# Mamba layer of a four-layer hybrid: a buffer for the logarithm, merged silus, other slots for the turning of states, another order for the first chunk

## The chip, the core and the metric

One core of one Trainium2 chip, float32 throughout. The time is device microseconds of one execution of the whole program. The core has five engines, each with its own in-order queue: TensorE (PE; its weight loads are the row PEld), VectorE (DVE), ScalarE (ACT), GpSimd (POOL) and SyncE (SP), whose queue issues most transfers.

## The reference, cut to what matters

The program computes four layers on an image tensor of 2 x 256 x 32 x 32: layer 0 is a pair of Mamba blocks, layer 1 a large-kernel convolution attention, layers 2 and 3 attention with mixtures of experts. Only layer 0 is touched by the change. It starts with a group norm, and then each Mamba block (512 inner channels, 16 states) does this on the 1024 tokens of each of two images:

```python
xs, res = split(u @ in_w + in_b)
xs = silu(conv4(xs) + conv_b)                   # depthwise, four taps, causal
dt, B, C = split(xs @ xproj_w)                  # 16 + 16 + 16
delta = softplus(dt @ dt_w + dt_b)
for t: h = exp(delta_t * A) * h + delta_t * B_t * xs_t ;  y_t = sum over states of h * C_t
y = (y + xs * D) * silu(res);  out = y @ out_w + out_b;  x = x + layernorm(out)
```

## The kernel before

Layer 0 is cut in chunks of 512 tokens: two blocks of four chunks, eight in a row, numbered 0 to 7 here. Chunks 0, 2, 4 and 6 begin an image (no state is read). Channels lie on partitions, as four groups of 128 (`dc` 0 to 3). Each chunk has three parts, written as Python generators that give up control at each `yield`:

- `front(j)`: input product (four groups, `m_in`), convolution as four matmuls by diagonal matrices (`taps`) for each group (`m_conv`), silu (L280), the product with `xproj_w` (`m_xd`), `m_ct` (the C columns), then softplus: |v| into `e` (L316) and relu into `delta` (L317) from PSUM, `e = exp(-e)` (L319, one instruction for all groups), a correction `du` for the rounding of 1 + e (L322, L323), the logarithm in place on `e` (L325), and three additions and products (L328 to L330) that leave delta and `du` = delta * xs. The elementwise steps of L322 to L330 go to POOL, those of chunk 0 to VectorE.
- `scan(j)`: for each state n of 16, `m_b` (one row of B on all partitions, fetched by SP), two halves h(n, 0) and h(n, 1) on POOL (L377, 128 x 1024), and for each group ACT's `m_da` = exp(delta * A) into PSUM (L384, three buffers) and VectorE's scan along time (L388), written scan (n, dc) here. Then each of four pieces of 128 tokens is turned by four PE transposes into PSUM (`m_ht`, L350, written ht(n, i), three buffers), and VectorE adds it, times C, to `m_ya` (L358; L356 for n = 0), written y(n, i). There are five buffers for the halves h, used in turn, and a half is free once all pieces of its n are turned.
- `back(j)`: gate product and silu (L408, L412), sum with the skip path (`m_y`), product with the gate (L427), output product (`m_out`), layer norm (L142 to L147), turning back (L153) and the addition to x (L454, L459).

`scan` weaves the others in. After each scan (n, dc) it takes one step of `between` (for n > 0 and dc < 3: three slots of four, none in n = 0) and then one step of `before`, which turns and adds one piece of the state before:

```python
if n and dc < 3:
    next(between, None)
next(before, None)
```

`between` is a chain: `back` of the last chunk, `front` of the next one, then seven steps of `aside` (small products for layer 1's taps: `w1t`, `taps_ps`). The framework's scheduler then settles each engine's final order when the program is built: it follows the order of writing, but puts an instruction that it holds ready ahead of one that it holds waiting. What stands where on each engine is read from the built program.

Pools that matter: `m_one` has one buffer a tag (`pre`, which is also `e`; `gate`; `o`), `m_mm` has two PSUM buffers for all small products, `m_da` three, `m_ht` three. An activation function from another table set than the last one needs a table load on ACT (`ACT_TABLE_LOAD`).

Before chunk 0, SP issues the loads in the order columns, rows, four tiles of x, weights; the group norm of both images runs, and then the front of chunk 0, alone.

Of the kernel before, what the change touches and what calls it, by code (L numbers as in the profile page):

```python
# [9 lines left out]
F32 = mybir.dt.float32  # L10
# [52 lines left out]
class Net:  # L63


    def __init__(self, ctx, tc, cols, rows):
        self.tc, self.nc = tc, tc.nc
        nc = self.nc
        const = ctx.enter_context(tc.tile_pool(name="const", bufs=1))
        self.small = ctx.enter_context(tc.tile_pool(name="small", bufs=4))  # L70
        self.cols = const.tile([P, NCOLS], F32, name="cols_sb")
        nc.sync.dma_start(self.cols, cols)
        self.rows = const.tile([P, NROWS], F32, name="rows_sb")
        nc.sync.dma_start(self.rows, rows.partition_broadcast(P))
        self.ident = const.tile([P, P], F32, name="ident")
        make_identity(nc, self.ident)
        self.eps5 = const.tile([P, 1], F32, name="eps5")
        nc.vector.memset(self.eps5, 1e-5)
        self.eps6 = const.tile([P, 1], F32, name="eps6")
        nc.vector.memset(self.eps6, 1e-6)  # L80
        self.one = const.tile([P, 1], F32, name="one")
        nc.vector.memset(self.one, 1.0)
        self.ones_row = const.tile([1, P], F32, name="ones_row")
        nc.vector.memset(self.ones_row, 1.0)

# [73 lines left out]
def group_norm(net, pool, psum, u, x):  # L159

    nc = net.nc
    grp = pool.tile([P, P], F32, name="gn_grp")
    nc.vector.memset(grp, 0.125)
    g3 = grp.rearrange("p (g j) -> p g j", j=8)
    nc.gpsimd.affine_select(
        out=g3, in_=g3, compare_op=ALU.is_ge, fill=0.0, base=0,
        pattern=[[-8, 16], [0, 8]], channel_multiplier=1,
    )
    nc.gpsimd.affine_select(
        out=g3, in_=g3, compare_op=ALU.is_ge, fill=0.0, base=7,  # L170
        pattern=[[8, 16], [0, 8]], channel_multiplier=-1,
    )
    n = NCC * NB
    mv = pool.tile([P, n, 2], F32, name="gn_mv")
    for cc in range(NCC):
        for b in range(NB):
            st = net.small.tile([P, 2, 6], F32, name="gn_st")
            for h in range(2):
                nc.vector.bn_stats(out=st[:, h, :], in_=x[:, cc, b, h * 512 : (h + 1) * 512])
            nc.vector.bn_aggr(out=mv[:, cc * NB + b, :], in_=st.rearrange("p h s -> p (h s)"))  # L180
    means = pool.tile([P, n], F32, name="gn_means")
    nc.vector.tensor_copy(means, mv[:, :, 0])
    ps = psum.tile([P, TC], F32, tag="mm", name="gn_ps")
    nc.tensor.matmul(ps[:, :n], lhsT=grp, rhs=means, start=True, stop=True)
    gm = pool.tile([P, n], F32, name="gn_gm")
    nc.vector.tensor_copy(gm, ps[:, :n])

    d = pool.tile([P, n], F32, name="gn_d")
    nc.vector.tensor_sub(d, means, gm)
    nc.vector.tensor_mul(d, d, d)  # L190
    nc.vector.tensor_add(d, d, mv[:, :, 1])
    ps = psum.tile([P, TC], F32, tag="mm", name="gn_ps2")
    nc.tensor.matmul(ps[:, :n], lhsT=grp, rhs=d, start=True, stop=True)
    rs = pool.tile([P, n], F32, name="gn_rs")
    net.rstd(rs, ps[:, :n])
    for b in range(NB):
        for cc in range(NCC):
            i = cc * NB + b
            nc.vector.tensor_scalar(
                u[:, cc, b, :], x[:, cc, b, :], gm[:, i : i + 1], rs[:, i : i + 1],  # L200
                ALU.subtract, ALU.mult,
            )


class Mamba:
# [10 lines left out]
    def load(self):  # L216
        net, nc, m, wpool = self.net, self.net.nc, self.m, self.wpool
        in_w, out_w, xproj_w, dt_w = self.weights
        self.in_sb = wpool.tile([P, NCC, DI], F32, tag="in_w", name=f"{m}_in_sb")
        nc.sync.dma_start(self.in_sb, in_w[:, :, :DI])  # L220
        self.xp_sb = wpool.tile([P, NDC, XD], F32, tag="xproj_w", name=f"{m}_xp_sb")
        nc.sync.dma_start(self.xp_sb, xproj_w)
        self.dt_sb = wpool.tile([RANK, DI], F32, tag="dt_w", name=f"{m}_dt_sb")
        nc.sync.dma_start(self.dt_sb, dt_w)
        self.gate_sb = wpool.tile([P, NCC, DI], F32, tag="gate_w", name=f"{m}_gate_sb", bufs=2)
        nc.sync.dma_start(self.gate_sb, in_w[:, :, DI:])
        self.out_sb = wpool.tile([P, NDC, C], F32, tag="out_w", name=f"{m}_out_sb", bufs=2)
        nc.sync.dma_start(self.out_sb, out_w)

        self.taps = wpool.tile([P, NDC * 4, P], F32, tag="taps", name=f"{m}_taps")  # L230
        self.skip = wpool.tile([P, NDC, P], F32, tag="skip", name=f"{m}_skip", bufs=2)
        for i in range(NDC * 4):
            nc.vector.tensor_scalar_mul(
                self.taps[:, i, :], net.ident, net.col(f"{m}_conv_w", i)
            )
        for dc in range(NDC):
            nc.vector.tensor_scalar_mul(self.skip[:, dc, :], net.ident, net.col(f"{m}_D", dc))
        self.aneg = wpool.tile([P, NDC * NS], F32, tag="aneg", name=f"{m}_aneg", bufs=2)
        nc.scalar.activation(self.aneg, net.col(f"{m}_A_log", 0, NDC * NS), AF.Exp)
        nc.vector.tensor_scalar_mul(self.aneg, self.aneg, -1.0)  # L240
        self.state = wpool.tile([P, NS, NDC], F32, tag="state", name=f"{m}_state", bufs=2)
# [5 lines left out]
    def front(self, j, eng=None):  # L247

        net, nc, m, one, two = self.net, self.net.nc, self.m, self.one, self.two
        eng = eng or nc.gpsimd  # L250
# [22 lines left out]
        for dc in range(NDC):  # L273
            ps = self.ps_mm.tile([P, TC], F32, tag="mm", name=f"{m}_conv_{j}_{dc}")
# [5 lines left out]
            nc.scalar.activation(xs[:, dc, :], ps, AF.Silu, bias=net.col(f"{m}_conv_b", dc))  # L280
# [4 lines left out]
        for dc in range(NDC):  # L285
            nc.tensor.matmul(
                ps[:XD, :], lhsT=self.xp_sb[:, dc, :], rhs=xs[:, dc, :],
                start=(dc == 0), stop=(dc == NDC - 1),
            )
        nc.scalar.copy(xd, ps[:XD, :])  # L290
# [16 lines left out]
        e = one.tile([P, NDC, 3 + TC], F32, tag="pre", name=f"{m}_e_{j}")[:, :, :TC]  # L307
        du = two.tile([P, NDC, TC], F32, tag="du", name=f"{m}_du_{j}")
        for dc in range(NDC):
# [7 lines left out]
            nc.scalar.activation(delta[:, dc, :], ps, AF.Relu, bias=b)  # L317
            yield
        nc.scalar.activation(e, e, AF.Exp, scale=-1.0)  # L319
# [5 lines left out]
        nc.scalar.activation(e, e, AF.Ln, bias=net.one)  # L325
        yield
        for dc in range(NDC):
            eng.tensor_add(e[:, dc, :], e[:, dc, :], du[:, dc, :])  # L328
            eng.tensor_add(delta[:, dc, :], delta[:, dc, :], e[:, dc, :])
# [4 lines left out]
    def scan(self, j, before, between):  # L334
# [11 lines left out]
        def add(n, hs, i):  # L346

            ps = self.ps_ht.tile([P, DI], F32, tag="ht", name=f"{m}_ht_{j}_{n}_{i}")
            for dc in range(NDC):
                nc.tensor.transpose(  # L350
                    ps[:, dc * P : (dc + 1) * P], hs[dc // G][:, dc % G, i * P : (i + 1) * P],
                    net.ident,
                )
            c = ct[:, i, n : n + 1]
            if n == 0:
                nc.vector.tensor_scalar_mul(ya[:, i, :], ps, c)  # L356
            else:
                nc.vector.scalar_tensor_tensor(ya[:, i, :], ps, c, ya[:, i, :], ALU.mult, ALU.add)  # L358

# [4 lines left out]
        def rest(n, hs):  # L364
            for i in range(TPC):
                if i == 1 and first:
                    keep(n, hs)
                add(n, hs, i)
                yield

        for n in range(NS):
# [9 lines left out]
            for dc in range(NDC):  # L381
# [9 lines left out]
                if n and dc < 3:  # L391
                    next(between, None)
                next(before, None)
            before = rest(n, hs)
# [4 lines left out]
    def back(self, j):  # L399
# [5 lines left out]
        for dc in range(NDC):  # L405
            ps = self.ps_mm.tile([P, TC], F32, tag="mm", name=f"{m}_g_{j}_{dc}")
            for kc in range(NCC):
# [5 lines left out]
                gate[:, dc, :], ps, AF.Silu, bias=net.col(f"{m}_in_b", NDC + dc)  # L413
            )
            yield

# [46 lines left out]
def layer0(net, x, x_dram, m1, m2, aside):  # L463
# [4 lines left out]
    with (  # L468
# [13 lines left out]
        ]  # L482
        blocks[0].load()
        group_norm(net, wpool, ps_mm, x, x)
        units = [(m, j) for m in blocks for j in range(NCH)]
        for _ in units[0][0].front(0, nc.vector):
            pass
        before, done = iter(()), []
        aside = aside(ps_mm)
        for u, (m, j) in enumerate(units):  # L490
            ahead = units[u + 1 : u + 2]
            if ahead and ahead[0][1] == 0:
                ahead[0][0].load()
            before = m.scan(j, before, chain(*done, *(a.front(k) for a, k in ahead), islice(aside, 7)))
# [5 lines left out]
class Taps:  # L500
# [3 lines left out]
    def __init__(self, net, pool, w1, w2):  # L504
# [3 lines left out]
        nc.sync.dma_start(self.w2_sb, w2)  # L508
# [743 lines left out]
def conv_attn_hybrid(ctx: ExitStack, tc: tile.TileContext, a: dict, out: bass.AP):  # L1252
# [7 lines left out]
    with (  # L1260
# [3 lines left out]
        for cc in range(NCC):  # L1264
            for b in range(NB):
                nc.sync.dma_start(x[:, cc, b, :], a["x"][b, cc])

# [5 lines left out]
            lambda psum: taps.make(psum, conv_dram),  # L1273
# [98 lines left out]
```

## Time and profile before

| | us |
|---|---|
| median of 9 runs | 2614.33 (2604.52 to 2619.06) |
| profiled execution | 2617.87 |
| its span | 2614.3 |
| first scan / first scan of state 1, group 1 | 75.18 / 81.69 |
| end of the last scan and accumulation of layer 0 | some 1204 |
| engines busy in the span: PE, DVE, ACT, POOL | 2140.6, 1479.9, 1033.7, 1068.7 |

The first accumulations of state 0 stand at 81.05, 217.14, 364.32, 507.73, 652.01, 794.22, 938.88 and 1080.60 us: a chunk takes 136 to 147 us. The profile is one execution. A wait is put down to what ended it; a line such as `DVE a L1 <- ACT b L2: 10.0, 4, 3.0` says that VectorE's instruction of line 1 waited 10.0 us for ACT's line 2, in four places, the longest 3.0. In a timeline the first two columns are start and duration in us, `x2` counts instructions put together, and brackets give the idle time before.

### The profile page before, as it was taken

To read this page: it belongs to the slowest core of one execution; us is meant where nothing else is said; L and a number is where in the kernel's file an instruction comes from. 1 tells how busy PE (TensorE), PEld (TensorE's weight loads), DVE (VectorE), ACT (ScalarE), POOL (GpSimd) and SP (SyncE) were. 2 spreads that over 40 slices of the span, in tenths; PEclk is the share of its full clock that TensorE was granted. 3 is DMA by queue.
4 is the path that set the end of the run, shared out by engine and by line. 5 is a ranking of instruction groups with operands and counts; after the bars stand their busy time and mean duration, and the time that the engine had idled before them with its cause. 6 is when DMAs were issued, how large, how long until landed. Compare 5 with 4: busy or idle time off the path is not lost. (4 is left out here: it accounts for less than half of the span.)

```text
span 2614.3 us, 24599 instructions
## 1 busy us (share of the span) xinstructions
PE 2140.6 (82%) x8178; PEld 1309.0 (50%) x8178; DVE 1479.9 (57%) x2232; ACT 1033.7 (40%) x1664; POOL 1068.7 (41%) x708
## 2 busy tenths in 40 slices
PE   5767778696868778777999789949999499689995
PEld 2445445454545454544555556526555267456653
DVE  2879789787979797995002865542222333522222
ACT  3764656666565757561001243312111423211113
POOL 0786766859595867662000620013232000023331
PEclk9767888797878878876998899969999799789997
DMA  3011101101111111110000010038888200178885
GB/s 140 29 47 33 31 33 53 38 27 50 29 49 40 45 37 34 48 53 1 11 6 1 1 41 8 17 141 304 286 291 279 77 1 17 73 250 311 312 283 177
DMA packets 74909, 241.87 MB, mean 93 GB/s; under 512 B 21944, under 2 KB 34621, under 8 KB 62624
## 3 DMA queue, kind: packets, MB, share of 16 engines
q1 hardware_dynamic: 65504, 219.32, 24.6%
q0 software_dynamic: 9024, 20.74, 2.6%
q8 instruction: 65, 1.06, 0.2%
q14 instruction: 60, 0.49, 0.1%
q10 hardware_dynamic: 256, 0.26, 0.0%
HBM read 222.87 MB, written 21.33 MB: 93 GB/s over the span
## 5 line engine op out<-in xcount | busy, mean ns | idle before, releaser
L377 POOL TENSOR_TENSOR m_h<-m_du,m_b 128x1024 f32<-128x1024 f32 x256 | 600.2, 2369 | 341.3 <-PE m_ht L350 157.0
L350 PE MATMUL m_ht<-ident,m_h 128*128 128x128 f32 x2048 | 417.5, 331 | 173.5 <-DVE m_ya L358 95.5
L350 PEld LDWEIGHTS m_ht<-ident,m_h 128*128 128x128 f32 x2048 | 282.2, 167 | 377.5 <-issue 116.9
L384 ACT ACTIVATE m_da<-m_delta,m_aneg 128x512 f32<-128x512 f32 x512 | 349.6, 690 | 265.0 <-DVE m_h L388 260.0
L358 DVE SCALAR_TENSOR_TENSOR m_ya<-m_ht,m_ct,m_ya 128x512 f32<-128x512 f32 x480 | 344.0, 729 | 60.6 <-PE m_ht L350 60.2
L1183 PE MATMUL h<-we,xts 128*128 128x512 f32 x752 | 343.8, 600 | 1.0 <-DVE xts L1173 1.0
L388 DVE TENSOR_TENSOR_SCAN m_h<-m_da,m_state,m_h 128x512 f32<-128x512 f32 x256 | 320.2, 1268 | 38.2 <-ACT m_da L384 26.6
L388 DVE TENSOR_TENSOR_SCAN m_h<-m_da,m_h 128x512 f32<-128x512 f32 x256 | 304.8, 1206 | 56.8 <-ACT m_da L384 37.7
L1155 POOL DMA_INDIRECT x<-l_zd,source x94 | 95.8, 1019 | 510.3 <-DVE source L1119 449.3
L1214 POOL DMA_INDIRECT yd<-y,target x94 | 95.6, 1017 | 347.3 <-DMA yd<-y,target 177.3
L1190 DVE TENSOR_TENSOR hid<-hid,h 128x512 f32<-128x512 f32 x94 | 64.6, 688 | 282.1 <-PE h L1183 282.1
L1183 PEld LDWEIGHTS h<-we,xts 128*128 128x128 f32 x752 | 137.5, 193 | 139.7 <-issue 137.9
L1201 ACT COPY hts<-ht 128x512 f32<-128x512 f32 x94 | 55.1, 586 | 351.0 <-PE ht L1197 351.0
L1208 PE MATMUL o<-we,hts 128*128 128x256 f32 x752 | 184.5, 390 | 1.5 <-ACT hts L1201 1.5
L604 PE MATMUL acc<-act,pair 128*98 128x448 f32 (+14 forms) x448 | 165.3, 517 | 0.0
L1208 PEld LDWEIGHTS o<-we,hts 128*128 128x128 f32 x752 | 139.7, 196 | 19.5 <-ACT hts L1201 1.9
L1213 DVE COPY y<-o 128x256 f32<-128x256 f32 x94 | 39.9, 424 | 149.6 <-DMA yd<-y,target 79.6
L276 PE MATMUL m_conv<-m_pre,m_taps 128*128 128x512 f32 x256 | 115.5, 594 | 3.3 <-ACT m_xs L280 3.2
L604 PEld LDWEIGHTS acc<-act,pair 128*98 128x98 f32 x448 | 73.8, 167 | 70.3 <-issue 54.2
L528 PE MATMUL taps_ps<-w_sb,w1ts 128*128 128x49 f32 x196 | 44.1, 385 | 69.5 <-ACT w1ts L524 69.3
L1189 ACT ACTIVATE hid<-h 128x512 f32<-128x512 f32 x94 | 56.1, 597 | 99.1 <-PE h L1183 98.0
L384 ACT ACT_TABLE_LOAD x69 | 88.5, 1283 | 1.2
(289 smaller groups left out, 3079.6 us busy)
## 6 DMA issues: line engine op xcount, KB each, us to landing
we<-in_l_experts_dram SPq DMA_DIRECT2D x94, 1536.0 KB, 8.4
m_b<-m_bd SPq DMA_DIRECT2D x128, 256.0 KB, 3.2
yl<-yd SPq DMA_DIRECT2D x16, 512.0 KB, 5.0
w<-in_l_w_dram SPq DMA_DIRECT2D x7, 896.0 KB, 6.2
l_zd<-l_z SPq DMA_DIRECT2D x8, 512.0 KB, 2.9
taps<-taps_sb SPq DMA_DIRECT2D x7, 343.0 KB, 3.5
pair<-taps SPq DMA_DIRECT2D x7, 343.0 KB, 3.9
act<-in_x_dram SPq DMA_DIRECT2D x4, 512.0 KB, 7.0
```

Source lines behind the costliest of these rows:

```text
L276: nc.tensor.matmul(ps, lhsT=self.taps[:, dc * 4 + k, :], rhs=pre[:, dc, k : k + TC], start=(k == 0), stop=(k == 3),)
L350: nc.tensor.transpose(ps[:, dc * P : (dc + 1) * P], hs[dc // G][:, dc % G, i * P : (i + 1) * P], net.ident,)
L358: nc.vector.scalar_tensor_tensor(ya[:, i, :], ps, c, ya[:, i, :], ALU.mult, ALU.add)
L377: nc.gpsimd.tensor_mul(h, du[:, g * G : (g + 1) * G, :], b.unsqueeze(1).to_broadcast(half))
L384: nc.scalar.activation(da, delta[:, dc, :], AF.Exp, scale=self.aneg[:, i : i + 1])
L388: nc.vector.tensor_tensor_scan(h, da, h, 0.0 if first else state[:, n, dc : dc + 1], ALU.mult, ALU.add)
L604: nc.tensor.matmul(acc[b, k][:, lo - 16 * k : hi - 16 * k, co : co + n], lhsT=lhsT, rhs=x4[:, kc, b, lo - r0 : hi - r0, ci : ci + n], star ...
L1155: nc.gpsimd.indirect_dma_start(out=x, out_offset=None, in_=zd[:, :], in_offset=bass.IndirectOffsetOnAxis(ap=source[:, g : g + 1], axis=0), ...
L1183: nc.tensor.matmul(ps, lhsT=xt[:, kc * P : (kc + 1) * P], rhs=w12[:, s, kc, :], start=(kc == 0), stop=(kc == NCC - 1),)
L1190: nc.vector.tensor_mul(hid, hid, h[1])
L1208: nc.tensor.matmul(ps[:, :C], lhsT=ht[:, mc * P : (mc + 1) * P], rhs=w[:, 8 + mc, :], start=(mc == 0), stop=(mc == NHC - 1),)
L1214: nc.gpsimd.indirect_dma_start(out=yd[:, :], out_offset=bass.IndirectOffsetOnAxis(ap=target[:, g : g + 1], axis=0), in_=y, in_offset=None, ...
```

## The change

Five edits, all in layer 0. Line numbers of the changed file are some 30 to 50 higher.

1. `ln = Ln(1 + e)` goes to a tile of its own, with the tag of `gate`, right behind the exponential; the correction steps read `e` and come behind it, with the two additions and the product.
2. The four evictions of the convolution and of the gate add their bias with `Identity`, and one `Silu` in place follows over all four groups. Chunk 0 keeps its silus apart.
3. `front` yields in the middle of each convolution group and of the xproj product, and twice for each group of the softplus steps; `scan` gives `between` a step after every scan but the very first.
4. `rest` makes the four transposes of a piece, yields, and adds the piece only when it is called again, after the next scan. `before` is called ahead of `between`, and what is left of the state before is chained.
5. Start: columns and `w2` are issued from ACT's queue, x of image 0 ahead of the weights, x of image 1 and the rows behind; the group norm works by image, that of image 1 behind chunk 0's front; the front of chunk 0 (`alone`) makes groups 1 and 3 of the convolution on VectorE, the relu on VectorE, and Exp and Ln by group.

```diff
 # scan
-                if n and dc < 3:
+                next(before, None)
+                if n or dc:
                     next(between, None)
-                next(before, None)
-            before = rest(n, hs)
+            before = chain(before, rest(n, hs))
 # rest
             for i in range(TPC):
-                if i == 1 and first:
+                ps = self.ps_ht.tile([P, DI], F32, tag="ht", name=f"{m}_ht_{j}_{n}_{i}")
+                for dc in range(NDC):
+                    nc.tensor.transpose(
...
+                yield
+                c = ct[:, i, n : n + 1]
...
+                    nc.vector.scalar_tensor_tensor(
+                        ya[:, i, :], ps, c, ya[:, i, :], ALU.mult, ALU.add
+                    )
+                if i == 0 and first:
                     keep(n, hs)
-                add(n, hs, i)
-                yield
 # front: convolution
+            if alone and dc % 2:
+                nc.vector.tensor_scalar(
...
+                for k in range(1, 4):
+                    nc.vector.scalar_tensor_tensor(
...
+                nc.scalar.activation(xs[:, dc, :], xs[:, dc, :], AF.Silu)
+                continue
...
+                if k == 1:
+                    yield
-            nc.scalar.activation(xs[:, dc, :], ps, AF.Silu, bias=net.col(f"{m}_conv_b", dc))
+            nc.scalar.activation(xs[:, dc, :], ps, AF.Silu if alone else AF.Identity, bias=b)
+            yield
+        if not alone:
+            nc.scalar.activation(xs, xs, AF.Silu)
             yield
 # front: softplus
+        ln = one.tile([P, NDC, TC], F32, tag="gate", name=f"{m}_ln_{j}")
...
-            nc.scalar.activation(delta[:, dc, :], ps, AF.Relu, bias=b)
+            if alone:
+                nc.vector.tensor_scalar(delta[:, dc, :], ps, b, 0.0, ALU.add, ALU.max)
+            else:
+                nc.scalar.activation(delta[:, dc, :], ps, AF.Relu, bias=b)
             yield
-        nc.scalar.activation(e, e, AF.Exp, scale=-1.0)
+        parts = [slice(dc, dc + 1) for dc in range(NDC)] if alone else [slice(0, NDC)]
+        for a in parts:
+            nc.scalar.activation(e[:, a, :], e[:, a, :], AF.Exp, scale=-1.0)
+        for a in parts:
+            nc.scalar.activation(ln[:, a, :], e[:, a, :], AF.Ln, bias=net.one)
         yield
         for dc in range(NDC):
             eng.tensor_scalar(du[:, dc, :], e[:, dc, :], 1.0, -1.0, ALU.add, ALU.add)
             eng.tensor_sub(du[:, dc, :], e[:, dc, :], du[:, dc, :])
             yield
-        nc.scalar.activation(e, e, AF.Ln, bias=net.one)
-        yield
-        for dc in range(NDC):
-            eng.tensor_add(e[:, dc, :], e[:, dc, :], du[:, dc, :])
-            eng.tensor_add(delta[:, dc, :], delta[:, dc, :], e[:, dc, :])
+            eng.tensor_add(ln[:, dc, :], ln[:, dc, :], du[:, dc, :])
+            eng.tensor_add(delta[:, dc, :], delta[:, dc, :], ln[:, dc, :])
             eng.tensor_mul(du[:, dc, :], delta[:, dc, :], xs[:, dc, :])
             yield
 # layer0
+        norm = GroupNorm(net, wpool, ps_mm, x)
         blocks[0].load()
-        group_norm(net, wpool, ps_mm, x, x)
+        load_image()
+        blocks[0].load_rest()
+        net.load_rows()
+        norm.image(0)
         units = [(m, j) for m in blocks for j in range(NCH)]
-        for _ in units[0][0].front(0, nc.vector):
+        for _ in units[0][0].front(0, alone=True):
             pass
+        norm.image(1)
```

## The prediction

> **What bounds the kernel now.** The change touches layer 0 alone, so I read that stretch, 0 to 1204 us of the span. First the table of windows: from 750 to 890 us, one chunk, VectorE is busy 121.32 of 140 us, PE 112.71, POOL 101.86, ACT 86.49. VectorE sets the pace there: a scan and an accumulation follow each other every 1.78 us (1.83 where a state is read), 64 times a chunk. Only what VectorE waits for can be won or lost. The list of waits of layer 0 (waiter, what ended the wait: total us, times, longest) says for whom it waits:
>
> ```profile
> POOL m_h L377 <- PE m_ht L350: 157.0, 43, 8.8
> ...
> DVE m_h L388 <- ACT m_da L384: 64.3, 11, 9.1
> ...
> DVE m_ya L358 <- PE m_ht L350: 60.2, 34, 5.5
> ACT m_e L325 <- POOL m_du L323: 57.5, 7, 9.0
> ...
> DVE m_du L322 <- ACT m_e L319: 35.5, 1, 35.5
> ...
> DVE m_h L388 <- POOL m_h L377: 24.2, 21, 2.9
> ```
>
> ACT's logarithm (L325, in place on e) waits 57.5 us for POOL to have read e, and the exponentials behind it in ACT's queue starve the scans. Then POOL's own timeline over one such place (start, us, line, count):
>
> ```profile
> 446.14 4.67 POOL L377 TENSOR_TENSOR m_h<-m_du,m_b 128x1024 f32<-128x1024 f32 x2 [1.89 <-PE m_ht L350]
> 450.79 3.81 POOL L322 TENSOR_SCALAR m_du<-m_e 128x512 f32<-128x512 f32 x2
> 454.56 2.32 POOL L323 TENSOR_TENSOR m_du<-m_e,m_du 128x512 f32<-128x512 f32 x2
> 456.85 3.81 POOL L322 TENSOR_SCALAR m_du<-m_e 128x512 f32<-128x512 f32 x2
> 460.62 2.31 POOL L323 TENSOR_TENSOR m_du<-m_e,m_du 128x512 f32<-128x512 f32 x2
> 462.88 4.66 POOL L377 TENSOR_TENSOR m_h<-m_du,m_b 128x1024 f32<-128x1024 f32 x2
> 467.50 2.31 POOL L328 TENSOR_TENSOR m_e<-m_e,m_du 128x512 f32<-128x512 f32 x2
> ```
>
> POOL is never idle from 450.79 to 495: while ACT waits for it, POOL is late with the halves h itself. VectorE in the same place:
>
> ```profile
> 457.20 0.72 DVE L358 SCALAR_TENSOR_TENSOR m_ya<-m_ht,m_ct,m_ya 128x512 f32<-128x512 f32 x1
> 467.01 1.22 DVE L388 TENSOR_TENSOR_SCAN m_h<-m_da,m_h 128x512 f32<-128x512 f32 x1 [9.09 <-ACT m_da L384]
> ...
> 484.99 2.34 DVE L388 TENSOR_TENSOR_SCAN m_h<-m_da,m_h 128x512 f32<-128x512 f32 x2 [1.50 <-POOL m_h L377]
> ```
>
> Going through VectorE's timeline chunk by chunk, its waits add up to 152.7 us: 93.2 around the logarithm in chunks 0 to 6 (13.3 each), 41.6 in the stretch of the next chunk's convolution in chunks 1 to 6 (7.3 each, 4.7 in chunk 2), 6.2 in chunk 0 for silus, 6.2 later in chunks for PE, 5.5 in chunk 7.
>
> **The change, part by part.** *Logarithm in a buffer of its own.* The 57.5 us of ACT go. What is late next is POOL: each chunk's softplus costs it, by the view of groups, 4 x (1.920 + 1.175 + 1.181 + 1.184 + 1.273) = 26.9 us (L322, L323, L328, L329, L330). Before, waiting for the logarithm split this: 12.2 us, two halves h, 8.4 us, a half, and so on. In the changed program's order these instructions stand in one block, 19 or all 20 in a row, between h(11,1) and h(12,1) (in chunk 0 between h(7,1) and h(8,0)), with nothing in between that feeds a scan. There are five h buffers, so POOL can be only so far ahead: h(11,1) and h(12,0) both need n=9 transposed. In the trace scan (10,1) starts at 443.13 and that release comes at 446.14, 3.0 later; in the new order it is again the scan, two accumulations and one set of transposes, 1.13 + 0.64 + 0.64 + 0.6 = 3.0. So h(12,1) is ready 3.0 + 3 x 2.37 + 26.9 = 37.0 us after scan (10,1) starts. VectorE could want it after nine pairs and one accumulation that is owed, 9 x 1.78 + 0.64 = 16.7 (17.1 with states): it waits 20.2 on the mean. The same rule on the old order, whose last late half h(14,1) ends at 488.56, gives 45.4 - 17 x 1.78 = 15.1 where the timeline shows 14.7; shrunk alike I take 19.6. Against 13.3 that is +6.3 a chunk, +44 in seven. Bounds: +30 if the accumulations that VectorE pulls forward hide 2 us of each, +55 if nothing is pulled forward. The new buffer shares the tag of gate: the next gate waits for POOL's last reading of ln, which stands before the halves that chunk needs anyway: nothing.
>
> *One silu for four.* In layer 0 the built program has 69 table loads for 143: 74 x 1.283 = 95 us of ACT go, and 15 passes over 2048 columns come, 1.92 to 2.0 each by the rows of Exp (L319) and Ln (L325) of that shape, 29 us. Neither is on the path except in chunk 0, where VectorE's 6.2 us of waits for da follow silu loads. A merged silu blocks ACT for 1.28 + 1.95 + 1.28 = 4.5 us in one piece; three da buffers cover 3 x 1.78 = 5.3, so it costs nothing; without one of these buffers it would cost 1 us at each of 15 places. The Trainium skill ("ScalarE: Activation LUTs", What ACT_TABLE_LOAD costs) counts 2.66 us for a switch, with a drain. By it ACT would save 197 us; the trace shows no such drain (a load at 326.98, the next activation at 328.27), and either figure is off the path.
>
> *Finer steps in all slots, transposes one slot ahead of their accumulation.* PE must still do 13.7 us of convolution in the stretch. By the rows of 405 to 435 us: three input products 6.2, the fourth 1.72, a convolution 3.44, now in halves of 1.72, four transposes 0.43 and 0.2 until VectorE may read. A half and a set take 2.15 against a pair's 1.78, eight times over, after a backlog from the input products. Writing the new PE order out by these rows, VectorE waits 1.5 for ht(4,3), 1.7 for h(6,1) and 1.4 for h(7,1), both held by PE, where the old order had 0.8, 1.3, 1.2, 3.4 and 0.6; the last two go since no xd product stands before a transpose in need. With the back's steps now denser (PE half a us later) I take 4.9 for six chunks: 29.4 - 41.6 = -12. Bounds 0 and -25. Chunk 0 gets such a stretch too, since its input products no longer run before the first scan: 4.5 - 6.2 = -2 (-6 to +2). The later PE waits of 6.2 go, as PE catches up in POOL's block, and about half of chunk 7's 5.5: -9 (-12 to 0).
>
> *First chunk reordered.* Before: x lands behind 1.28 MB at 7.5, PE starts at 20.7, xd ends at 46.95, Abs starts at 49.2, the first h ends at 75.15, scan (1,1) starts at 81.69. After: x of image 0 behind 0.65 MB (5.6), two tiles of statistics to 8.7, taps and skips 4.1 of VectorE in the way as before, image 1's statistics between the small steps, the norm in halves: PE starts at 17.9. Two of four convolutions go to VectorE (2.5 us each, beside PE): PE does 16 passes of 0.43 fewer, and with the shorter tail xd ends at 37.0, Abs starts at 39.2. Then by parts: ten short activations at 0.6 and five table loads at 1.28, with VectorE's additions between, the last but one addition at 55.8. The first h is slow in the trace:
>
> ```profile
> 69.42 5.73 POOL L377 TENSOR_TENSOR m_h<-m_du,m_b 128x1024 f32<-128x1024 f32 x1 [38.79 <-DVE m_du L330]
> ```
>
> It ends 2.37, its usual time, after VectorE's last additions at 72.94, so I let the new one run only after 55.8: 58.2. The four first scans, image 1's norm (1.7) and ACT's square root with two loads put scan (1,1) at 67.9. That is 13.8 earlier, with one accumulation of 0.64 still owed: -13 (-17 if h runs beside the additions, -8 if every part waits for the one before it). The Trainium skill ("SBUF — State Buffer", SBUF: two separate sides) says that VectorE with two SBUF inputs and a reading GpSimd lock each other out; the 5.73 agrees, and it speaks against additions by parts beside the first h: by the rule the gain is the 13 above, without it 17.
>
> **The sum.** -13 + 44 - 12 - 2 - 9 = +8. The profiled execution took 2617.87 us (span 2614.3); it would be 2626. The median of the runs is 2614.33, 3.5 below it: I predict 2622.5.
>
> **The rivals.** *Faster.* PE's half steps keep the transposes ahead and the waits of the convolution stretch fall to 1.5 a chunk: -32 instead of -12; with POOL's block at the lower 5.3 a chunk (+37) the sum is -19, 2595. For it: 3.4 of the 7.3 is one wait for the long xd product. Against it: PE's work there is unchanged, and POOL's 157 us of waiting for m_ht shows the halves hang on PE. It decides if those waits are under 3 us a chunk. *Slower still.* ACT now has Abs and Relu of four tiles, Exp and Ln in one burst (some 6, then 4.6 us), and Exp ends only 1.9 us before POOL's block wants it. If it comes 3 us late, each chunk loses 3 more: +29, 2643. For it: four L316 waits for m_dt of 0.8 to 1.5 in the trace. *Cancelling.* The block costs +38 and the start and PE parts give 38: 2614. *Not what it says:* nothing is left out of the work; the logarithm's wait goes for certain, only POOL's queue decides what that is worth.
>
> **How the numbers follow.** Forecast 0.5 (own range 2612 to 2634), cancelling 0.15, faster 0.2, slower still 0.15. Some 0.2%, 5 us, is what runs of this kernel can tell from no change. Slower by more: 0.36 of the forecast's half, 0.05 of the cancelling case, and 0.15: 0.56. Faster by more: 0.2 and 0.02 of the cancelling case: 0.22. Same: 0.14 and 0.08: 0.22. The range reaches to both outer cases: 2594 to 2644.
>
> **What would show it.** Right: the waits of ACT for POOL (57.5) and most of VectorE's 64.3 for ACT gone; VectorE's wait for POOL m_h up from 24 to over 120, in seven pieces of 14 to 20; POOL's softplus instructions in a row of 26 us; scan (1,1) near 68; convolution waits of some 5 a chunk. Wrong: a piece under 13 us per chunk at POOL's block, the chunk pitch (143 now) under 141, or the first scan after 65.

## The result and the profile after

The changed kernel is slower: 2628.01 us, median of 21 runs (2619.53 to 2642.38), where the kernel before has 2610.4 on the same chips (63 runs). The ratio is 1.0069, 95% interval 1.0053 to 1.0085, some 18 us; 8 were forecast. The profiled execution took 2633.25 us (span 2631.6).

What the change can reach ends where layer 1's first product starts on PE; I call that the handover. It moved from 1231.6 to 1256.8 us, 25.2 later. In the list of waits of layer 0 (waiter, what ended the wait: total us, times, longest) the waits have changed places as forecast:

```profile
DVE m_h L425 <- POOL m_h L414: 139.4, 26, 19.0
...
DVE m_ya L402 <- PE m_ht L393: 26.4, 25, 2.3
...
DVE m_h L425 <- ACT m_da L421: 16.4, 9, 4.0
```

ScalarE's 57.5 us of waiting for GpSimd are gone, and VectorE's wait for ScalarE fell from 64.3 to 16.4. Its wait for GpSimd's halves h rose from 24.2 to 139.4. GpSimd's timeline in chunk 2 (start, us, line, count, idle time before):

```profile
443.48 2.36 POOL L414 TENSOR_TENSOR m_h<-m_du,m_b 128x1024 f32<-128x1024 f32 x1 [0.95 <-issue]
445.80 3.92 POOL L362 TENSOR_SCALAR m_du<-m_e 128x512 f32<-128x512 f32 x2
449.69 2.43 POOL L363 TENSOR_TENSOR m_du<-m_e,m_du 128x512 f32<-128x512 f32 x2
452.09 3.81 POOL L362 TENSOR_SCALAR m_du<-m_e 128x512 f32<-128x512 f32 x2
...
470.37 1.28 POOL L366 TENSOR_TENSOR m_delta<-m_delta,m_ln 128x512 f32<-128x512 f32 x1
471.58 2.36 POOL L414 TENSOR_TENSOR m_h<-m_du,m_b 128x1024 f32<-128x1024 f32 x1
```

From 445.80 to 471.58 there is no half h: 25.8 us, 19 softplus steps in a row. VectorE at the same place:

```profile
444.47 3.35 DVE L234 TENSOR_SCALAR m_taps<-ident,cols_sb 128x128 f32<-128x128 f32 x7
447.40 1.21 DVE L425 TENSOR_TENSOR_SCAN m_h<-m_da,m_h 128x512 f32<-128x512 f32 x1
448.53 2.62 DVE L234 TENSOR_SCALAR m_taps<-ident,cols_sb 128x128 f32<-128x128 f32 x6
...
457.99 1.37 DVE L402 SCALAR_TENSOR_TENSOR m_ya<-m_ht,m_ct,m_ya 128x512 f32<-128x512 f32 x2
473.98 2.34 DVE L425 TENSOR_TENSOR_SCAN m_h<-m_da,m_h 128x512 f32<-128x512 f32 x2 [14.62 <-POOL m_h L414]
```

It has used up all halves at 459.4 and stands until 473.98. Six more such pieces stand in chunks 0 to 6: 15.31, 19.00, 19.01, 15.29, 19.00 and 15.28. The short ones are those of chunks 0, 4 and 6, with 4.0 us for ScalarE's da ahead of them, and this one. The two rows of L234 are the taps of the second block, the diagonal matrices of its convolution; they return below.

### The profile page after: what moved, and what is told of

The parts are those of the page before. It is cut to its first block, busy times and chain, and to the rows that moved or that the text cites. A ratio compares the mean times of both kernels' runs of the same rounds, so it can differ in the third digit from the quotient of the medians.

```text
span 2631.6 us, 24530 instructions
## 1 busy us (share of the span) xinstructions
PE 2126.9 (81%) x8166; PEld 1315.5 (50%) x8166; DVE 1501.8 (57%) x2252; ACT 964.4 (37%) x1608; POOL 1076.3 (41%) x708
## 3 DMA queue, kind: packets, MB, share of 16 engines
q1 hardware_dynamic: 65216, 219.18, 24.4%
## 5 line engine op out<-in xcount | busy, mean ns | idle before, releaser
L393 PEld LDWEIGHTS m_ht<-ident,m_h 128*128 128x128 f32 x2048 | 300.0, 173 | 463.6 <-issue 182.5
L447 PE MATMUL m_g<-act,m_gate_sb 128*128 128x512 f32 x128 | 78.1, 699 | 39.3 <-ACT taps_sb L579 39.3
```

Source lines behind the costliest of these rows:

```text
L393: nc.tensor.transpose(ps[:, dc * P : (dc + 1) * P], hs[dc // G][:, dc % G, i * P : (i + 1) * P], net.ident,)
L447: nc.tensor.matmul(ps, lhsT=self.gate_sb[:, kc, dc * P : (dc + 1) * P], rhs=xt[:, kc, tok], start=(kc == 0), stop=(kc == NCC - 1),)
```

## The experiments

All kernels ran against the kernel before. Beside the ratio I give the handover, and VectorE's waits from the timelines in two sums: the convolution stretch (the first 72 us of chunks 1 to 6, counted from the first accumulation) and the time behind it, where the softplus stands (chunks 0 to 6; chunk 0 from 52 us on). Each wait of over 0.15 us counts once, where the instruction that waited starts. The diffs are cut to the lines that matter.

**Is the block the cause? Fewer softplus steps on GpSimd.** The first kernel leaves out the rounding correction.

```diff
-            eng.tensor_scalar(du[:, dc, :], e[:, dc, :], 1.0, -1.0, ALU.add, ALU.add)
-            eng.tensor_sub(du[:, dc, :], e[:, dc, :], du[:, dc, :])
-            yield
-            eng.tensor_add(ln[:, dc, :], ln[:, dc, :], du[:, dc, :])
```

> The changed kernel with the rounding correction of the softplus left out (the steps e+1-1, e-du and ln+du, on GpSimd for chunks 1 to 7), so that its result lacks that correction; all other edits stay. GpSimd's softplus block falls from 20 to 8 instructions, by 4 x (1.92 + 1.18 + 1.18) = 17.1 us a chunk. Theory 'block' (VectorE starves because the whole block lies between two halves h): the 15 to 19 us pieces fall to 0 to 3, some 16 us in each of seven chunks, layer 0 ends 105 to 115 us earlier, ratio to the kernel before 0.962 to 0.967. Theory 'ScalarE burst' (Exp, logarithm and their table loads in one run of 6.5 us starve the scans): only chunk 0 gains, ratio 1.000 to 1.007. Theory 'slots' (the new order of transposes and half convolutions holds VectorE): also 1.000 to 1.007.

Ratio 0.9682 (0.9647 to 0.9718), handover 1162.2. VectorE's waits for GpSimd:

```profile
DVE m_h L421 <- POOL m_h L410: 20.1, 15, 1.5
```

139.4 became 20.1, no piece over 1.5, and the waits behind the convolution stretch fell from 142.3 to 40.0. Layer 0 ends 94.6 us earlier, somewhat less than the 105 to 115 expected; the other two theories allowed next to no gain. So GpSimd's steps between two halves are what VectorE waits for in the changed kernel. That the change made this worse by putting them in one row is the matter of the partial edits further on. The next kernel moves two of the five steps to VectorE and leaves nothing out.

```diff
-            eng.tensor_scalar(du[:, dc, :], e[:, dc, :], 1.0, -1.0, ALU.add, ALU.add)
-            eng.tensor_sub(du[:, dc, :], e[:, dc, :], du[:, dc, :])
+            nc.vector.tensor_scalar(du[:, dc, :], e[:, dc, :], 1.0, -1.0, ALU.add, ALU.add)
+            nc.vector.tensor_sub(du[:, dc, :], e[:, dc, :], du[:, dc, :])
```

> The changed kernel with e+1-1 and e-du (two of five correction steps for each group) on VectorE instead of GpSimd in all chunks; nothing is left out. GpSimd's block falls by 4 x (1.92 + 1.18) = 12.4 us, VectorE gets 4 x (0.34 + 0.60) = 3.8 us of work, most of it in time in which it waited. Theory 'block': the wait of 19 falls to 19 - 12.4 - 3.8 = 3, and 3.8 of work is paid, 12 us less in each of seven chunks: 85 us, ratio 0.972 to 0.978. If VectorE's two-input steps slow down beside a busy GpSimd (2.71 us for 0.68 was seen once in chunk 0), up to 8 us a chunk come back: ratio 0.985 to 0.995. Rivals 'slots' and 'ScalarE burst': VectorE only gets more work, ratio 1.015 to 1.02.

Ratio 0.9779 (0.9743 to 0.9814), handover 1189.0; the waits behind the stretch fell to 24.4. The full computation is now faster than in both kernels, but at the far end of what was expected (67.8 us of layer 0 and not 85). The groups of VectorE (line, count, busy us, mean ns) show why:

```profile
L362 DVE TENSOR_SCALAR m_du<-m_e 128x512 f32<-128x512 f32 x28 | 37.6, 1372 | 0.0
L363 DVE TENSOR_TENSOR m_du<-m_e,m_du 128x512 f32<-128x512 f32 x28 | 22.8, 834 | 0.0
```

8.6 us a chunk instead of 3.8. The step with one input suffers most: 0.42 us in chunk 0, here 0.393 to 2.577, on the mean 1.372. The scans and accumulations kept their 1.21 and 0.73. Next, ScalarE makes 1 + e, and VectorE has one step for each group instead of two.

```diff
-            nc.scalar.activation(ln[:, a, :], e[:, a, :], AF.Ln, bias=net.one)
+            nc.scalar.activation(du[:, a, :], e[:, a, :], AF.Identity, bias=net.one)
...
+            nc.scalar.activation(ln[:, a, :], du[:, a, :], AF.Ln)
...
-            eng.tensor_scalar(du[:, dc, :], e[:, dc, :], 1.0, -1.0, ALU.add, ALU.add)
-            eng.tensor_sub(du[:, dc, :], e[:, dc, :], du[:, dc, :])
+            nc.vector.scalar_tensor_tensor(
+                du[:, dc, :], du[:, dc, :], -1.0, e[:, dc, :], ALU.add, ALU.subtract)
-            eng.tensor_add(ln[:, dc, :], ln[:, dc, :], du[:, dc, :])
+            eng.tensor_sub(ln[:, dc, :], ln[:, dc, :], du[:, dc, :])
```

> The changed kernel with 1 + e made once by ScalarE (Identity with a bias of one, 1.92 us for all groups), the logarithm taken of it, and the correction as one step (t-1)-e for each group on VectorE; GpSimd keeps three steps a group, 14.5 us. Nothing is left out. Before it, with two correction steps on VectorE, the single-input step e+1-1 took 1.37 us on the mean where it takes 0.42 alone, and the two-input step 0.83. Theory 'the single-input steps pay for GpSimd being busy': VectorE has 4 x 0.83 = 3.3 instead of 8.6 us a chunk, the waits stay at 5 to 11 a chunk, so 30 to 37 us less than that version (2555): 2518 to 2530, ratio 0.963 to 0.970. Rival 'any VectorE work here pays alike': ratio 0.974 to 0.978.

Ratio 0.978 (0.9735 to 0.9826), handover 1188.3: the rival's. The step with two inputs pays as well, 1.42 us on the mean and up to 2.83, not the 0.83 of the theory, though it is still less than the pair's 2.21:

```profile
L364 DVE SCALAR_TENSOR_TENSOR m_du<-m_du,m_e 128x512 f32<-128x512 f32 x28 | 38.6, 1424 | 3.7 <-ACT m_ln L361 3.6
```

So VectorE saved 21.8 us in seven chunks. Against that, the waits behind the stretch rose from 24.4 to 32.3, and chunk 0, where the sum had also gone to ScalarE, lost 6.7 us (first accumulation at 77.4, not the changed kernel's 70.7). The next kernel takes all four groups in one step, gives chunk 0 its old way back and moves the taps to ScalarE.

```diff
+            nc.vector.scalar_tensor_tensor(du, du, -1.0, e, ALU.add, ALU.subtract)   # all four groups
...
-            nc.vector.tensor_scalar_mul(self.taps[:, i, :], net.ident, ...)
+            nc.scalar.activation(self.taps[:, i, :], net.ident, AF.Identity, scale=...)
```

> The changed kernel, chunk 0's softplus as it is there, and in the other chunks 1 + e on ScalarE and the correction (t-1)-e as one instruction over all four groups on VectorE (it was four, 1.42 us on the mean beside a busy GpSimd, 0.66 at the least), 12 steps on GpSimd; the diagonal taps are made by ScalarE instead of VectorE (16 steps took 10.9 us in chunk 2 where the kernel before has 3.3). Nothing is left out. Theory 'VectorE waits for GpSimd once for each instruction, whatever its length': the step costs 2.2 us and one wait of about 1 instead of 5.7, 2.5 less in seven chunks, 17; the taps give 11, chunk 0 gives back 6.7: some 35 us below the 2558 of the version with four steps, 2523, ratio 0.960 to 0.969. Rival 'the loss goes with the data that it reads': only 17 us from taps and chunk 0, ratio 0.970 to 0.975.

Ratio 0.9743 (0.969 to 0.9795), handover 1180.4, 8 before the last one; 35 were expected. Each part did what it should: the step costs 2.6 us a chunk instead of 5.5,

```profile
L371 DVE SCALAR_TENSOR_TENSOR m_du<-m_du,m_e 128x2048 f32<-128x2048 f32 x7 | 18.1, 2587 | 3.4 <-ACT m_ln L369 3.4
```

20.5 in seven chunks, the taps' 10.9 us have left VectorE, and the first accumulation came 7.9 earlier: 39 in all. But the waits behind the stretch rose from 32.3 to 53.5, and the others by 8.5, so most of the gain was given back; the ratio lies in the rival's range, though the row above speaks against the rival's reason. Of the 53.5, ScalarE ended 33.3, where it had been 3.4. About half of that, the longest pieces (4.7, 4.6, 3.9, 2.3 and 1.5), comes right behind a wait of ScalarE's own:

```profile
ACT m_gate L460 <- POOL m_delta L375: 39.2, 6, 9.0
```

ScalarE's gate shares the logarithm's buffer and has to wait until GpSimd has read it for the last time; the exponentials behind it in ScalarE's queue, and VectorE's scans, wait along. With four steps this wait was 8.8 us, in the changed kernel there is none. What a buffer of its own would bring back here was not run.

```diff
-                next(before, None)
-                if n or dc:
+                if n and dc < 3:
                     next(between, None)
+                next(before, None)
```

> The same with edits 3 and 4 undone (old slots, a piece turned and added in one step). In the changed kernel undoing them brought layer 0's end 17 us forward. Theory 'the new slots are worse because they bring the softplus block early into a starving window': without a long block little is left of it, ratio within 0.003 of the version with the new slots. Rival 'the new slots cost by themselves': 12 to 20 us below it, ratio 0.005 to 0.008 lower.

Ratio 0.975 (0.9694 to 0.9806), handover 1177.5, 3 us before the other: the first theory's. By the handover these two are the fastest with the full computation.

**What did each edit bring?** One part alone, or one undone:

```diff
 # own_buffer_alone, in the kernel before
+        ln = one.tile([P, NDC, TC], F32, tag="gate", name=f"{m}_ln_{j}")
+        nc.scalar.activation(ln, e, AF.Ln, bias=net.one)
```

> The kernel before with the logarithm's own buffer and nothing else of the change. On GpSimd the softplus steps stand as 9, 4, 5 and 2 with one half h between each, not as 19 or 20 in a row. Theory 'block, by the same rule': 18 of 20 steps stand ahead of h(13,1), 24 us; that half is ready 3.0 + 5 x 2.37 + 24 = 38.9 us after scan (10,1) starts and is wanted after 16.7 + 4 x 1.78 = 23.8, a wait of 15.1, shrunk as before to some 14.6 against 13.3: +1.3 a chunk, +9 us, ratio 1.002 to 1.006. Rival 'the 57.5 us that ScalarE waited for GpSimd were on the path': faster by 30 us or more, ratio below 0.989.

Ratio 0.9982 (0.9958 to 1.0006), handover 1231.6, to 0.1 us that of the kernel before. ScalarE's 57.5 us of waiting have gone (16.9 come back at the gate, which shares the buffer), and VectorE's list shows in their place

```profile
DVE m_h L388 <- POOL m_h L377: 92.7, 37, 5.9
```

where the kernel before had 24.2 for GpSimd and 64.3 for ScalarE. The 57.5 us were on no path of their own: GpSimd was late anyway. And alone the buffer costs nothing, where the rule had 9 us: here the steps still stand as 9, 4, 5 and 2 (or 8, 6, 5 and 1), halves between. The nothing is made of two parts: the first accumulation comes 3.9 us earlier (77.17 for 81.05), and from there to the last one it takes 4.4 longer.

```diff
 # in_place, in the changed kernel
-            nc.scalar.activation(ln[:, a, :], e[:, a, :], AF.Ln, bias=net.one)
...
+            nc.scalar.activation(e[:, a, :], e[:, a, :], AF.Ln, bias=net.one)   # behind the corrections
```

> The changed kernel with the logarithm in place on e again, behind the correction steps; all other edits stay. Theory 'block': ScalarE's wait for GpSimd returns and splits the softplus steps on GpSimd into 8 and 12 with two halves h between; the waits around the logarithm fall from 19.0 a chunk (measured in the changed kernel) back to 13 to 14, 35 to 42 us less, ratio 0.991 to 0.994. Rival 'slots or merged silu cost it': the ratio stays at 1.005 to 1.009. Rival 'the buffer helps and another edit cost more': the ratio rises to 1.02.

Ratio 0.9983 (0.9962 to 1.0005), handover 1240.3: 16.5 us of the 25 came back, not 35 to 42. (Chunk 0 starts 4.0 later without the buffer, so from the first accumulation on it is 20.8.) VectorE's waits:

```profile
DVE m_h L426 <- POOL m_h L415: 97.1, 26, 8.6
DVE m_h L426 <- ACT m_da L422: 39.2, 8, 10.6
```

The waits behind the stretch stay at 17.8 a chunk, not 13 to 14: with the new slots the steps stand as 8 and 12, in the kernel before as 8, 10 and 2 or in shorter rows (8, 6 and 6).

```diff
 # old_slots, in the changed kernel: scan and rest as in wide_step_old_slots; in front these go
-                if k == 1:            # convolution
-                    yield
-            if dc == 1:               # xproj product
-                yield
-            yield                     # between correction and addition
```

> The changed kernel with edits 3 and 4 undone: steps of front as coarse as before, three slots of four, a piece turned and added in one step; the logarithm's buffer, the merged silus and the new start stay. The softplus block of 18 to 20 steps stands one half later, between h(12,1) and h(13,0). Theory 'block, by the rule': h(13,0) is ready 3.0 + 2 x 2.37 + 26.9 = 34.6 us after scan (11,1) starts and wanted after 7 x 1.78 + 0.64 + what is owed, some 13 to 16, so the waits around the logarithm are no shorter than the 19.0 of the changed kernel, up to 20.5; the waits of the convolution stretch, 46 us in the changed kernel and 48 before, do not change: ratio 1.006 to 1.012. Rival 'the new slots themselves cost' (in place with the new slots, the waits around the logarithm were 17 to 18 a chunk where the kernel before had 13): 4 us a chunk come back, ratio 0.995 to 1.001.

Ratio 0.9995 (0.9969 to 1.0021), handover 1240.0. The waits behind the stretch are 19.9 a chunk, within the rule's 19.0 to 20.5, but those of the stretch fell from 29.9 to 20.7, in chunk 7 from 2.5 to none. So the rival is right on the time: the new slots cost 17 us.

```diff
 # start_alone, in the kernel before: edit 5, in layer0
         blocks[0].load()
-        group_norm(net, wpool, ps_mm, x, x)
+        load_image()
+        blocks[0].load_rest()
+        net.load_rows()
+        norm.image(0)
-        for _ in units[0][0].front(0, nc.vector):
+        for _ in units[0][0].front(0, alone=True):
             pass
+        norm.image(1)
```

> The kernel before with edit 5 alone: the new order of loads, the group norm by image, chunk 0's front with two convolution groups and the relu on VectorE, Exp and the logarithm by group (in place); slots, silus and buffers of the other chunks as before. In the changed kernel the first accumulation stood at 70.7 us, 10.3 earlier than before. Theory 'the start's gain is kept to the end of layer 0': the other chunks are the same, so layer 0 ends 9 to 11 us earlier, ratio 0.995 to 0.997. Rival 'chunk 0 gives it back, because the next chunk's input products no longer lie ahead of its first scan': chunk 0 is 5 to 10 longer, ratio 0.998 to 1.000.

Ratio 0.9947 (0.9922 to 0.9972), handover 1219.8: 11.8 us, kept to the end of layer 0.

```diff
 # silus_apart, in the changed kernel
-            nc.scalar.activation(xs[:, dc, :], ps, AF.Silu if alone else AF.Identity, bias=b)
+            nc.scalar.activation(xs[:, dc, :], ps, AF.Silu, bias=b)
-        if not alone:
-            nc.scalar.activation(xs, xs, AF.Silu)
-            yield
...                                  # the gate likewise
```

> The changed kernel with edit 2 undone: a silu for each of the four evictions again, so some 74 more table loads of 1.28 us on ScalarE. GpSimd's softplus steps then stand as 12 (4 in one chunk) ahead of h(10,1) and 8 (16) behind it. Theory 'block, and ScalarE has room': the sum of block waits is 3.0 + 4 x 2.37 + 26.9 - 20.3 = 19.1 by the rule where the changed kernel has 20.2; table loads cost nothing: ratio 1.002 to 1.008. Rival 'the merged silus are worth something because loads delay m_da': 2 to 4 us a chunk more, ratio 1.012 to 1.018.

Ratio 1.0106 (1.0068 to 1.0143), handover 1271.9, 15.1 later: between the two. The waits of the convolution stretch are 54.8 instead of 29.9, those behind it 132.0 instead of 142.3. The trace shows PE with no gap over 0.22 us from 547 to 590 there: the xproj and delta products follow the convolution at once, while PE is still behind with the transposes; in the changed kernel the merged silu stands between them and PE catches up (idle 1.90 and 1.27 at 572 to 574). By the profile PE ended 29.9 of the 54.8, GpSimd 24.8 and ScalarE none, which speaks against table loads that hold up `m_da`. That the delay of the products is what helps is still argued, not shown: no run moves it alone.

| edits made | handover | stretch | behind it | longest row of softplus steps (mean of seven chunks) |
|---|---|---|---|---|
| none | 1231.6 | 38.0 | 102.9 | 8 to 10 (8.7) |
| buffer | 1231.6 | 39.1 | 104.1 | 8 or 9 (8.6) |
| start | 1219.8 | 39.4 | 99.3 | 8 to 10 (8.7) |
| buffer, silus, start | 1240.0 | 20.7 | 139.4 | 12 to 20 (18.3) |
| silus, slots, start | 1240.3 | 30.4 | 124.5 | 12 (12) |
| buffer, slots, start | 1271.9 | 54.8 | 132.0 | 11 to 16 (13.6) |
| all | 1256.8 | 29.9 | 142.3 | 19 or 20 (19.4) |

The prices don't add up: the buffer is worth 0 alone and costs 16.5 with all others. What they share is the last column, the number of softplus steps that stand on GpSimd with no half h between: the three kernels with short rows wait 99 to 104 us behind the stretch, and from there the waits rise with the mean row, 124.5, 132.0, 139.4 and 142.3. Buffer, silus and slots each move the halves among the steps, so what one costs depends on the others.

**The same kernels again.**

> The kernel before, unchanged, for a second profile. Layer 0 handed over at 1231.6 us, and layers 1 to 3 took 1382.7 in the first profile, where nine other kernels with the same code in these layers took 1361 to 1375. Theory 'one execution's chance in the later layers': handover at 1230 to 1233, later layers 1362 to 1377. Rival 'the later layers are slower in the kernel before': 1380 to 1386.

> The changed kernel, unchanged, for a second profile. Layer 0 handed over at 1256.8 us in the first. Theory 'layer 0 is the same in every execution': 1255 to 1259, the five pieces of VectorE's wait for h of 15 to 19 us again in chunks 0 to 6. Rival 'layer 0 varies by as much as the medians leave open (25 in the profiles, 17.6 in the medians)': 1248 to 1252.

Handover 1232.2 and 1256.2, so layer 0 repeats within 0.6 us and the change costs it 24 to 25. The seven pieces repeat within 0.02 us; chunk 7's wait of 2.5 is gone in the second profile, and chunk 0 has 2.4 more. The later layers took 1362.8 and 1364.2, where the first profile of the kernel before had 1382.7: chance of one execution, most of it in layer 2's first stage with experts (374.7 us against 356 to 364 in all the others). The seven us between layer 0's 24 to 25 and the 18 (14 to 22) of the medians stay open.

## Why the prediction was right, and where not

Direction, mechanism and place were right, the size less than half of what came. By its own steps, in layer 0 (the kernel before against the changed one):

- **The block** (step of the logarithm's buffer). Forecast 19 or 20 instructions of 26.9 us in a row, seven pieces of 14 to 20, over 120 us of waiting: 25.8 us, 14.6 to 19.0, 139.4. Forecast +44 less the 6 of later PE waits, 38; the waits behind the stretch went from 102.9 to 142.3, +39.4. The tag that the buffer shares with the gate was put at nothing, and in the changed kernel no gate waits for GpSimd; in other orders it does (16.9 us with the buffer alone, 39.2 in wide_step).
- **The start.** Scan (1,1) at 69.57 for 67.9: 12.1 earlier than before, less the 0.6 of the accumulation that is owed, -11.5 for -13, and kept (start_alone). (One reading was off by little: the first h of the kernel before ended 2.2 us behind VectorE's additions, not 2.37.)
- **The convolution stretch.** The waits left were right, 29.9 for 29.4. The -12 was mis-sized on its other side: by the same cut the kernel before had 38.0 there and not 41.6, so it is -8.1. Chunk 0's new stretch has 7.4 for 6.2, +1.2 instead of -2. And the reason given was wrong: the new slots cost there (20.7 without them), the silus bring it.
- **Chunk 7**: 5.5 to 2.5, the -3 of the forecast (none in the second profile).
- **Merged silus "cost nothing" and bring nothing off chunk 0**: this step fell. Undone they cost 15 us, by the trace through PE in the convolution stretch.
- **Not in the sum: the taps.** The change adds no arithmetic there, but the 16 rows that build the second block's taps moved. Before, they stand at 429.85 to 433.7, where GpSimd runs nothing; now they lie between 417.7 and 451.2, each beside a GpSimd instruction. Groups of VectorE, before and after:

```profile
L233 DVE TENSOR_SCALAR m_taps<-ident,cols_sb 128x128 f32<-128x128 f32 x16 | 3.3, 277 | 0.1
```

```profile
L234 DVE TENSOR_SCALAR m_taps<-ident,cols_sb 128x128 f32<-128x128 f32 x16 | 10.9, 764 | 0.0
```

  7.6 us in chunk 2. The dearest two took 2.01 and 2.38 and end with the two halves h that GpSimd makes at the time (VectorE, then GpSimd):

```profile
417.71 4.31 DVE L234 TENSOR_SCALAR m_taps<-ident,cols_sb 128x128 f32<-128x128 f32 x2
417.29 4.65 POOL L414 TENSOR_TENSOR m_h<-m_du,m_b 128x1024 f32<-128x1024 f32 x2 [2.53 <-PE m_ht L393]
```

  Chunk 2's length beside the mean of chunks 1 and 3 went from -2.3 to +4.9 us, and with the taps on ScalarE (wide_step) it is +1.6. The diff does not touch these lines' cost; only the order on VectorE against GpSimd's shows it.

Together -11.5 + 39.4 - 8.1 + 1.2 - 3.0 + 7.6 = 25.6; the last accumulation moved from 1204.0 to 1230.0, 26.0. Against the forecast's 8 the 25.6 is 17.6 more: 7.6 from the taps, 3.9 from the stretch, 3.2 from chunk 0, 1.5 from the start, 1.4 from the block. So the block, which carried the argument, was sized within 2 us, and the forecast's total missed by what lay beside it.

The rivals: "faster" needed under 3 us of PE waits a chunk, and the stretch has 5.0. "Slower still" had +29 and layer 0 came to +26, but not for its reason: Exp ended at 444.12 in chunk 2, before GpSimd turned to the block at 445.80, and in none of the seven chunks did GpSimd wait for it. "Cancelling" fell with the start and PE parts, which gave 21 and not 38.

## What to carry to other kernels

A wait that ends is worth only what the engine behind it can then do: list that engine's new queue and count how long it does nothing for the pacing engine, against what its buffers let it be ahead. What helped here was not to remove the wait but to take steps off GpSimd (2 to 3% with the full computation). And when an edit reorders two engines, price every row that now stands beside the other one, also rows that the edit does not name.

## What was not expected of the hardware

A VectorE step from SBUF to SBUF beside a busy GpSimd costs up to one GpSimd instruction more, whatever its own length: 0.42 to at most 2.577 us (one input, 128x512), 0.28 to 2.38 (the taps), 0.66 to 2.83 (two inputs), where a half h takes 2.37. In correction_on_dve 19 of the 28 one-input steps were slow, and each of them ends 0.28 us behind the end of a GpSimd instruction. Scans and accumulations, with one input in PSUM, kept their 1.21 and 0.73. Not every GpSimd instruction does it: beside L362, which has one input, seven of the taps took 0.25 to 0.27.

One instruction over 2048 columns (wide_step) pays once. In four of seven chunks no GpSimd instruction ran beside it, and it took 2.29; in three it began beside a half h and took 2.85 to 3.16, and the next half, begun meanwhile, took 4.4 instead of 2.37. So GpSimd waits as well. The Trainium skill ("SBUF — State Buffer", SBUF: two separate sides) calls the shared port pair an exclusive lock that whoever starts first holds for the whole instruction, for VectorE steps in a two-port mode or with two SBUF inputs; the rows beside two-input GpSimd instructions agree, those beside L362 don't show it, and the forecast used it for the two-input additions alone and overlooked the one-input rows.
